# Slots of 511 rows instead of 383, and 42 instead of 44 node columns by slots and list, in a segment-max graph layer

## The chip, the cores and the metric

The kernel runs on one core of one Trainium2 chip. The metric is the device time of one execution in microseconds (us); the time before is 703.79 us, the median of 3 runs (703.43 to 704.61). A difference of 0.2% is 1.4 us.

## The reference, cut to what matters

There are 6250 nodes with 256 features each and 100,000 edges, sorted by their target `dst`. For every edge a message is made from its two ends, every node takes the maximum over the messages that arrive, and a layer norm follows.

```python
theta_x = (x[dst] - x[src]) @ theta_w.T + theta_b
phi_x = x[src] @ phi_w.T + phi_b
e = relu(theta_x + phi_x)
out = segment_max(e, dst, num_segments=6250)
out = where(isfinite(out), out, 0.0)
return layernorm(x + out)          # over the 256 features, no scale and no shift
```

The part of a message that depends on the target is the same for all of a node's edges. So it is enough to find, for every node, the maximum of B[src] over its edges, where B = x @ (phi_w - theta_w).T, and to add the target's part, the bias, the relu and the norm once per node.

## The kernel before, in words

**B.** TensorE (PE) makes the 6250 rows of B from transposed blocks of x (lines 771 to 815), and they are stored in DRAM as `b_rows`. Transposed x of the later nodes is kept in DRAM too (`x_columns`), for the end.

**Three ways to the maxima.** The nodes fall into two parts. The last P * TILES = 128 * 44 nodes (`OWN`, 5632 of them) are part 2; 44 consecutive nodes belong to each partition. The other `N1` = 618 nodes are part 1.

- *Part 1, by steps.* The first 128 * `FIRST_STEPS` edges are cut into 128 runs of 81 consecutive edges, one run to a partition. A step takes one edge of every run: GpSimd (POOL) gathers 128 rows of B into a `g` tile with one indirect DMA (`gather`, line 527, issued on line 528), and VectorE (DVE) does a running maximum that a cap cuts off where the node changes (line 696). Steps come in groups of 8 (`STEPS`) that fill one of five ring tiles (`RING`). The first two groups (`X_GROUPS`) gather x instead, before B is there. Each group is stored to `maxima_1`.
- *Part 2, by slots.* The 6250 rows of B are cut into slots of `SLOT_ROWS` = (KB - 1) * 128 + 127 = 383 rows: 16 full ones of three blocks and a last one of 122 rows in one block. For each slot, `choice` (line 1027) takes for every node of part 2 the lowest row of B in that slot among its edges of rank below 24 (`CHOICE_R`), two slots a batch, in int16 on DVE. The chosen row numbers are stored (`chosen_rows`) and read back broadcast to all partitions (`want`, line 1149). `make_hots` (line 1144) turns them into one-hot columns: an Abs and a Relu on ScalarE (ACT, lines 1157 and 1160), or one comparison on DVE for the first block (line 1155). `slot_halves` (line 1099) multiplies the slot's rows, split into two fp32r terms (`terms`), by the one-hot columns (line 1120), chunk by chunk of `CW` = 1024 nodes, in matmuls of 512 columns. A chunk has two halves of 128 features. A half's product is copied into `acc` for slot 0 (ACT, line 1132), and merged by a maximum for the others (DVE, line 1134).
- *Part 2, by list.* Edges that no slot took are packed into a list of 128 runs of `LIST_CHUNK` = 256 edges: `list_pieces` (line 1247) closes the gaps in eleven rounds on DVE (lines 1278 to 1288), stores `list_words`, and fetches each run again with three indirect DMAs (`gather_run`, line 540, each followed by a filler `iota` into `pause`). The list is then run like part 1: 256 gathers (`gather_2`, line 1346), 256 running maxima, stored to `maxima_2`; one last step carries over (line 694).

**Order.** Work is interleaved by hand (lines 1543 to 1665) and every engine works through its own queue in order. POOL's indirect DMAs are put in one order by `in_turn`: x, part 1, the three run gathers, the list (with the fix of part 1's heads, the list's carry and part 1's places between), part 2's places. From the 13th list piece on (`held`), each second gather waits for the running maximum that was queued last but one (`hold`, line 537). `halves_until` (line 1601) spreads the halves that are left evenly over the list's steps, all but those of `LAST_CHUNKS` parts. DVE's running maxima stay two groups (`LEAD`) behind the gathers.

**End.** When the list's maxima are stored, POOL gathers each node's row of `maxima_2` (one gather for each of the 44 columns), and shares of 8, 4 and 2 columns are finished: target's part on PE (line 1400), transposed `acc` (line 1409), maximum, sum and norm on DVE and ACT, store.

If a check on counts fails on the device, a general path sorts the edges and runs after all this (line 1671). It doesn't run here.

Of the kernel before, what the change touches and what calls it, by code (L numbers as in the profile page):

```python
# [39 lines left out]
FP = mybir.dt.float32  # L40
# [23 lines left out]
R = 36  # L64
ROWS = 127
KB = 3
SLOT = 512
DVE_HOTS = 1
SPREAD = 0.97
PAUSE = 160  # L70
CHOICE_R = 24
WORD = 1 << 13
# [363 lines left out]
def gnn_kernel(ctx: ExitStack, tc: tile.TileContext, x, src, dst, theta_w, theta_b, phi_w, phi_b, out):  # L436
# [19 lines left out]
    assert D == 2 * P and LEFT1 > 0 and OWN % 512 == 0 and TILES < 64 and P * T1 < E and WINDOW < E  # L456
    assert (P - 1) * T + 1 < E <= P * T and N < ID_MASK and P * T <= EDGES and E + 8 * P <= EDGES
    assert SLOT * NS <= slot_code(WORD - 1) < 1 << 15 and N < WORD and WORD << TABLE_BITS == 1 << 23 and SLOT == 1 << SLOT_BITS and P == 1 << P_BITS and SLOT_ROWS < SLOT and KB == 3 and ROWS == P - 1 and WINDOW <= 8 * P and OWN_LIST * P < 1 << 20
    BATCH_S = 2
    assert STEPS == 1 << STEPS_BITS and 3 * BATCH_S * CHOICE_R * TILES // 2 + TR <= 6 * WINDOW and LIST_CHUNK + 1 == LIST and LIST_CHUNK % STEPS == 0 and 3 * (BACK + LIST_CHUNK) <= WINDOW and BACK == R - 2 and CARRY_GROUPS * STEPS >= BACK and BACK + LIST_CHUNK <= OWN_LIST and R == 36 and CHOICE_R == 24 and OWN_LIST <= 512 and 1536 < TR <= 1536 + OWN_LIST  # L460

# [45 lines left out]

    pause = const.tile([P, PAUSE], FP, name="pause")
    latest = [None]
# [209 lines left out]
    slots = body.enter_context(tc.tile_pool(name="slots", bufs=2))  # L719
    weights = const.tile([P, KC, 2, D], FP, name="weights")  # L720

    bias_terms = const.tile([P, D], FR, name="bias_terms")
    pick = const.tile([P, P], FR, name="pick")
    with (
# [5 lines left out]
    ):  # L730
        w_in = prep.tile([P, 2, KC, D], FP, name="w_in")
        for i, w in enumerate((phi_w, theta_w)):
            nc.sync.dma_start(w_in[:, i], w.rearrange("(c p) k -> p c k", p=P))
        biases = prep.tile([P, 2, D], FP, name="biases")
        nc.vector.tensor_sub(w_in[:, 0], w_in[:, 0], w_in[:, 1])
        for i in range(2):
            for c in range(KC):
                ps = ps_t.tile([P, 2, KC, P], FP, name="ps_xt")
                for k in range(KC):
                    nc.tensor.transpose(ps[:, 0, k, :], w_in[:, i, c, k * P : (k + 1) * P], ident)  # L740
                weights_made = nc.vector.tensor_copy(weights[:, :, i, c * P : (c + 1) * P], ps[:, 0])
                if i == 1:
                    behind_in_order(weights_made, window_found[0], "search ahead of theta")
# [38 lines left out]
        def b_of(to, rows, kept=None):  # L782

            n = rows.shape[1]
            x_t = x_transposed(rows)
            if kept is not None:
                nc.sync.dma_start(kept, x_t[:, :n].rearrange("p h k n -> p (h k n)"))
            ps = ps_b.tile([P, 2, D], FP, name="ps_b")
            for h in range(n):
                for k in range(KC):  # L790
                    nc.tensor.matmul(  # L791
                        ps[:, h, :], x_t[:, h, k, :], weights[:, k, 0, :], start=(k == 0), stop=(k == KC - 1)
                    )
            nc.scalar.copy(to, ps[:, :n, :])  # L794
# [123 lines left out]
    def heads_1(capped):  # L918
        carry = misc()
        for k in range(KC):  # L920
            one = nc.tensor.transpose(carry[:, k * P : (k + 1) * P], capped[:, k, :], ident)
            behind_in_order(one, latest_product[0], "slots ahead of the heads")
        carried = work.tile([P, D], FP, name="carried", bufs=1)
# [4 lines left out]
        in_turn(iota(pause, 1, 0, 0))  # L928
        yield
# [11 lines left out]
    by_node = "p (j r) -> p j r"  # L941
    words, work_1, work_2, order = (table(n) for n in ("words", "work_1", "work_2", "order"))
    word = words.bitcast(I32)
# [3 lines left out]
    )  # L947
    behind_in_order(iota(order, 1, 1, 0), windows_fetched[0], "runs ahead of the ranks")
    padded, unused = table("padded", I16), table("unused", I16)
# [77 lines left out]
    def choice(s0):  # L1027
# [71 lines left out]
    def slot_halves(s, c):  # L1099
# [13 lines left out]
        for h in range(KC):  # L1113
            ps = ps_fetch.tile([P, CW], FP, name="ps_f")
            ps = ps[:, :wide_of]
            n = blocks * PARTS
            for i in range(n):
                b, part = divmod(i, PARTS)
                for w in range(0, wide_of, 512):
                    one = nc.tensor.matmul(  # L1120
                        ps[:, w : w + 512],
                        terms[:, part, b, h * P : (h + 1) * P],
                        hot[:, b, w : w + 512],
                        start=(i == 0),
                        stop=(i == n - 1),
                    )
# [3 lines left out]
            to = acc[:, h, begin : begin + wide_of]  # L1130
            if s == 0:
# [115 lines left out]
    def list_pieces():  # L1247
# [9 lines left out]
        node_ends = lambda row: row.rearrange(by_node, r=R)[:, :, R - 1]  # L1257
        nc.vector.tensor_tensor(up_to[:, 1:], node_ends(order), node_ends(before_it), op=ALU.subtract)
        yield
# [5 lines left out]
        )  # L1265
        distance = order.bitcast(I32)
        nc.vector.scalar_tensor_tensor(distance, empty, 0.5, before_it, op0=ALU.is_lt, op1=ALU.mult)
# [7 lines left out]
        for i in range((TR - 1).bit_length()):  # L1275
# [4 lines left out]
            )  # L1280
            if shift == 512:
                far = slice(3 * shift, TR)
                behind = slice(2 * shift, TR - shift)
                nc.vector.tensor_scalar(
                    moves[:, behind], done[:, far], 20 + i, 1, op0=ALU.logical_shift_right, op1=ALU.bitwise_and
                )
                nc.vector.copy_predicated(done[:, behind], moves[:, behind], done[:, far])
            one = nc.vector.copy_predicated(done[:, :n], moves[:, :n], done[:, shift : shift + n])  # L1288
# [14 lines left out]
        iota(edge, 1, 0, 0)  # L1303
        list_edges, second, third = (dst_w[:, i * n_run : (i + 1) * n_run] for i in range(3))
        for i, to in enumerate((list_edges, second, third)):
# [53 lines left out]
    def rows_of(part, j0, n, ps_tile):  # L1359
# [18 lines left out]
        def piece(k):  # L1378
            w = min(2, n - k)
            if part == 2:  # L1380
                j = j0 + k
                if j % 4 == 0:
                    x_tiles[0] = kept_ring.tile([P, 4 * KC, P], FP, name="kept")
                    rows = x_columns[:, j * KC * P : (j + 4) * KC * P]
                    nc.sync.dma_start(x_tiles[0], rows.rearrange("p (j n) -> p j n", n=P))
                x_t = x_tiles[0][:, j % 4 * KC :]
# [11 lines left out]
            for i in range(w):  # L1398
                for c in range(KC):
                    nc.tensor.matmul(  # L1400
                        a[:, i, :], x_t[:, 2 * i + c, :], weights[:, c, 1, :], start=False, stop=(i == w - 1 and c == KC - 1)
                    )
# [152 lines left out]
    for i, _ in enumerate(list_pieces()):  # L1555
# [8 lines left out]
        else:  # L1564
            fetch_parts(1)
    list_carry()
# [76 lines left out]
    assert widths[0] * P == CW  # L1643
    given, halves_of_tile = [0], []

    def by_turns():
# [4 lines left out]
        if not halves_of_tile:  # L1651
            both = ps_fetch.tile([P, CW], FP, name="ps_f")
            halves_of_tile.extend([both[:, : 2 * D], both[:, 2 * D :]])
        return halves_of_tile.pop(0)
# [47 lines left out]
```

## Time and profile before

| | us |
|---|---|
| median of 3 runs | 703.79 |
| the profiled execution's own time | 703.84 |
| its span in the profile | 702.0 |
| PE busy, weight loads aside | 650.7 |
| DVE busy | 627.0 |
| ACT busy | 513.2 |
| POOL busy | 438.1 |
| running maxima on DVE (line 696, 335 of them) | 161.1 |
| merges of slot products on DVE (line 1134, 192) | 216.4 |

Busy time of an engine leaves out issuing and waiting. POOL's 438.1 us are therefore not all the time for which its queue is taken: between two indirect DMAs that follow each other stands a gap that the profile calls "issue". A stage is best read by itself, since the stages have different limits: B until about 84 us, part 1 with the making of the list until about 225, the list until 598, and the end.

### The profile page before, as it was taken

To read this page: it belongs to the slowest core of one execution; us is meant where nothing else is said; L and a number is where in the kernel's file an instruction comes from. 1 tells how busy PE (TensorE), PEld (TensorE's weight loads), DVE (VectorE), ACT (ScalarE), POOL (GpSimd) and SP (SyncE) were. 2 spreads that over 40 slices of the span, in tenths; PEclk is the share of its full clock that TensorE was granted. 3 is DMA by queue.
4 is the path that set the end of the run, shared out by engine and by line. 5 is a ranking of instruction groups with operands and counts; after the bars stand their busy time and mean duration, and the time that the engine had idled before them with its cause. 6 is when DMAs were issued, how large, how long until landed. Compare 5 with 4: busy or idle time off the path is not lost.

```text
span 702.0 us, 9583 instructions
## 1 busy us (share of the span) xinstructions
PE 650.7 (93%) x2908; PEld 532.1 (76%) x2908; DVE 627.0 (89%) x1200; ACT 513.2 (73%) x597; POOL 438.1 (62%) x424
## 2 busy tenths in 40 slices
PE   4899978879798999999999999999999999999991
PEld 3688866657577788888888888888888878888881
DVE  6999999999998778989889897889888898979996
ACT  1345668989888877868778786779877687863596
POOL 6800178888813757777777677777667776057720
PEclk9899989989999999999999999999999999999996
DMA  8898563656645747868697689788887776655775
GB/s 249 293 350 322 191 187 109 204 192 210 215 174 182 260 150 255 266 225 284 209 319 241 219 302 332 230 247 280 307 267 262 247 235 208 206 170 162 261 292 206
DMA packets 61308, 167.04 MB, mean 238 GB/s; under 512 B 11944, under 2 KB 21953, under 8 KB 55233
## 3 DMA queue, kind: packets, MB, share of 16 engines
q1 hardware_dynamic: 40005, 106.89, 43.9%
q0 software_dynamic: 18976, 52.35, 25.1%
q10 hardware_dynamic: 2268, 7.11, 2.8%
q8 instruction: 25, 0.41, 0.3%
q14 instruction: 34, 0.28, 0.1%
HBM read 102.94 MB, written 63.36 MB: 237 GB/s over the span
## 4 chain that ended last, share of the span: by engine, by line
PE 61%; DVE 16%; ACT 7%; POOL 6%; issue 5%; DMA 4%; ACTq 0%; SPq 0%; DVEq 0%; POOLq 0%
PE ps_f L1120 58%; POOL g L528 6%; DVE words L1005 2%; ACT hot L1157 2%; ACT x_f L1458 2%; ACT hot L1160 2%; DMA g<-b_rows,src 1%; DVE work L1002 1%; DVE g L696 1%; ACT squares L1443 1%; DVE wide L1038 1%; DVE x_f L1414 1%; PE ps_e L1400 1%; DMA dst_w<-in_dst_dram,window 1%; DVE g L1410 1%
## 5 line engine op out<-in xcount | busy, mean ns | idle before, releaser
L1120 PE MATMUL ps_f<-hot,terms 128*128 128x512 f32 x2156 | 508.1, 396 | 18.8 <-DVE hot L1155 10.5
L1120 PEld LDWEIGHTS ps_f<-hot,terms 128*128 128x128 f32 x2156 | 406.6, 190 | 113.8 <-ACT hot L1160 14.6
L528 POOL DMA_INDIRECT g<-b_rows,list_src x256 | 262.4, 1025 | 107.8 <-issue 52.2
L1157 ACT ACTIVATE hot<-want,minus_row 128x1024 fp32r<-128x1024 f16 (+1 forms) x214 | 219.3, 1074 | 99.1 <-PE ps_f L1120 98.9
L1134 DVE TENSOR_TENSOR acc<-acc,ps_f 128x1024 f32<-128x1024 f32 x192 | 216.4, 1129 | 49.7 <-PE ps_f L1120 47.8
L1160 ACT ACTIVATE hot<-hot 128x2048 fp32r<-128x2048 f32 (+2 forms) x102 | 188.8, 1851 | 2.4
L696 DVE SCALAR_TENSOR_TENSOR g<-g,caps 128x256 f32<-128x256 f32 x335 | 161.1, 481 | 1.7
L528 POOL DMA_INDIRECT g<-b_rows,src x65 | 92.3, 1420 | 66.5 <-DMA b_rows<-b_sb 47.1
L791 PE MATMUL ps_b<-weights,x_t 128*128 128x256 f32 x260 | 63.7, 400 | 7.6 <-ACT x_t L779 7.2
L528 POOL DMA_INDIRECT g<-maxima,place x44 | 42.2, 960 | 33.7 <-DMA maxima<-g 20.6
L791 PEld LDWEIGHTS ps_b<-weights,x_t 128*128 128x128 f32 x260 | 50.4, 200 | 16.7 <-ACT x_t L779 10.1
L1155 DVE TENSOR_SCALAR hot<-want,row_id 128x1024 fp32r<-128x1024 f16 x80 | 56.9, 712 | 0.0
L794 ACT COPY b_sb<-ps_b 128x512 f32<-128x512 f32 (+1 forms) x25 | 14.4, 579 | 30.8 <-PE ps_b L791 21.1
L1400 PE MATMUL ps_e<-weights,kept 128*128 128x256 f32 x144 | 34.0, 379 | 0.0
L1443 ACT ACTIVATE squares<-x_f,r 128x256 bf16<-128x256 f32 x47 | 23.2, 494 | 12.5 <-DVE r L1440 12.5
L1400 PEld LDWEIGHTS ps_e<-weights,kept 128*128 128x128 f32 x144 | 27.3, 190 | 3.6
L528 POOL DMA_INDIRECT g<-in_x_dram,src x16 | 21.1, 1320 | 5.4 <-issue 4.1
L779 ACT COPY x_t<-ps_xt 128x512 f32<-128x512 f32 (+1 forms) x33 | 18.3, 590 | 7.8 <-PE ps_xt L776 7.6
L1458 ACT ACTIVATE x_f<-x_f,r 128x256 f32<-128x256 f32 x40 | 20.6, 587 | 4.6 <-DVE r L1450 4.6
L1288 DVE COPY_PREDICATED work<-words,work 128x316 int32<-128x316 int32 (+9 forms) x11 | 18.2, 1659 | 0.0
L1414 DVE SCALAR_TENSOR_TENSOR x_f<-g,x_f 128x256 f32<-128x256 f32 x44 | 17.1, 423 | 0.3
L1038 DVE TENSOR_TENSOR wide<-wide 128x88 int16<-128x88 int16 (+5 forms) x45 | 16.2, 360 | 1.3
(273 smaller groups left out, 405.8 us busy)
## 6 DMA issues: line engine op xcount, KB each, us to landing
maxima<-g SPq DMA_DIRECT2D x41, 1024.0 KB
want<-chosen_rows SPq DMA_DIRECT2D x85, 256.0 KB
x_q<-in_x_dram SPq DMA_DIRECT2D x12, 512.0 KB
b_rows<-b_sb ACTq DMA_DIRECT2D x12, 512.0 KB
x_columns<-x_t SPq DMA_DIRECT2D x22, 256.0 KB
kept<-x_columns SPq DMA_DIRECT2D x11, 512.0 KB
raw<-b_rows SPq DMA_DIRECT2D x16, 256.0 KB
g<-b_rows,list_src POOLq DMA_INDIRECT x256, 4.9
```

What stands on the lines that cost most here:

```text
L528: one = nc.gpsimd.indirect_dma_start(out=to, out_offset=None, in_=table, in_offset=bass.IndirectOffsetOnAxis(ap=offsets, axis=0))
L696: one = nc.vector.scalar_tensor_tensor(g[:, k, :], last[part], caps[:, t : t + 1], g[:, k, :], op0=ALU.min, op1=ALU.max)
L791: nc.tensor.matmul(ps[:, h, :], x_t[:, h, k, :], weights[:, k, 0, :], start=(k == 0), stop=(k == KC - 1))
L1120: one = nc.tensor.matmul(ps[:, w : w + 512], terms[:, part, b, h * P : (h + 1) * P], hot[:, b, w : w + 512], start=(i == 0), stop=(i == n ...
L1134: one = nc.vector.tensor_tensor(to, to, ps, op=ALU.max)
L1155: nc.vector.tensor_scalar(hot[:, b, :], want, row_id[:, b : b + 1], None, op0=ALU.is_equal)
L1157: nc.scalar.activation(hot[:, b, :], want, AF.Abs, bias=minus_row[:, b : b + 1], scale=1.0)
L1160: nc.scalar.activation(apart, apart.bitcast(FP), AF.Relu, bias=1.0, scale=-1.0)
L1400: nc.tensor.matmul(a[:, i, :], x_t[:, 2 * i + c, :], weights[:, c, 1, :], start=False, stop=(i == w - 1 and c == KC - 1))
L1414: one = nc.vector.scalar_tensor_tensor(y, m[:, i, :], 0.0, y, op0=ALU.max, op1=ALU.add, accum_out=totals[:, i : i + 1])
L1443: nc.scalar.activation(squares, x_f[:, k, :], AF.Square, bias=mean[:, k : k + 1], scale=1.0, accum_out=var[:, k : k + 1])
L1458: nc.scalar.activation(x_f[:, k, :], x_f[:, k, :], AF.Identity, bias=mean[:, k : k + 1], scale=inv[:, k : k + 1])
```

## The change

Constants first. Slots get four blocks (`KB`), so 511 rows: 12 full ones and a last one of 118 rows. Part 2 has 42 columns (5376 nodes), cut into six chunks of 896, each in two matmuls of 448 columns that stand at the starts of two PSUM banks. Part 1 has 874 nodes and 112 steps in 14 groups. The list has 304 steps and one that carries over. Ranks below 20 are offered to the slots.

```diff
-AHEAD_OF_RUNS = 3
+AHEAD_OF_RUNS = 2
-FIRST_STEPS = 81
+FIRST_STEPS = 112
-TILES = 44
-LIST = 257
-WINDOW = 872
+TILES = 42
+LIST = 305
+WINDOW = 848
-KB = 3
+KB = 4
-PAUSE = 160
-CHOICE_R = 24
+CHOICE_R = 20
-LAST_CHUNKS = 10
+LAST_CHUNKS = 9
-OWN_LIST = 316
-LIST_CHUNK = 256
+OWN_LIST = 368
+LIST_CHUNK = 304
...
-    CW = 1024
+    CW = 896
```

The filler after each run gather and after the gather of heads goes:

```diff
         indirect(to, flat(table, 0, [[total, 1], [1, total]]), bass.IndirectOffsetOnAxis(ap=offsets, axis=1))
-        in_turn(iota(pause, 1, 0, 0))
```

The matmuls of a half:

```diff
-            ps = ps_fetch.tile([P, CW], FP, name="ps_f")
-            ps = ps[:, :wide_of]
+            ps = ps_fetch.tile([P, 2, 512], FP, name="ps_f")
+            half = wide_of // 2
+            ps = ps[:, :, :half]
...
-                for w in range(0, wide_of, 512):
+                for w in range(2):
                     one = nc.tensor.matmul(
-                        ps[:, w : w + 512],
+                        ps[:, w, :],
                         terms[:, part, b, h * P : (h + 1) * P],
-                        hot[:, b, w : w + 512],
+                        hot[:, b, w * half : (w + 1) * half],
```

The choice over 20 ranks, its minimum taken in five steps as before:

```diff
-        least(low, in_slot[:, :n, : 12 * W], in_slot[:, :n, 12 * W :])
-        least(low[:, :, : 6 * W], low[:, :, : 6 * W], low[:, :, 6 * W :])
-        least(low[:, :, : 3 * W], low[:, :, : 3 * W], low[:, :, 3 * W : 6 * W])
+        least(low, in_slot[:, :n, : 10 * W], in_slot[:, :n, 10 * W :])
+        least(low[:, :, : 5 * W], low[:, :, : 5 * W], low[:, :, 5 * W :])
+        least(low[:, :, : 2 * W], low[:, :, : 2 * W], low[:, :, 2 * W : 4 * W])
         least(low[:, :, :W], low[:, :, :W], low[:, :, W : 2 * W])
-        least(low[:, :, :W], low[:, :, :W], low[:, :, 2 * W : 3 * W])
+        least(low[:, :, :W], low[:, :, :W], low[:, :, 4 * W : 5 * W])
```

In the loop over the list's pieces, an odd piece brings one half instead of two while groups of part 1 are left. In the list's round of distance 512 the two instructions for far elements go (lines 1284 and 1287). At the end, `widths` loses its last share of 2:

```diff
-            fetch_parts(1)
+            fetch_half()
+            if len(groups_1) == 0 and i < 13:
+                fetch_half()
...
-    while halves_left[0] > 2 * (len(CHUNKS) - 1):
+    while halves_left[0] > 2 * (len(CHUNKS) - 2):
...
-    widths = [STEPS] * 3 + [4, 4, 4, 4, 2, 2]
+    widths = [STEPS] * 3 + [4, 4, 4, 4, 2]
```

Otherwise, phi's transposed weights stand in a tile of the first stage (`weights_b`), the table `order` shrinks to one number per column (`node_top`), and two buffers take the place of others that are done with.

More of the change, by code (lines that the diff above doesn't have):

```diff
@@ L731, in gnn_kernel @@
         w_in = prep.tile([P, 2, KC, D], FP, name="w_in")
+        weights_b = prep.tile([P, KC, D], FP, name="weights_b")
         for i, w in enumerate((phi_w, theta_w)):
@@ L922, in heads_1 @@
             behind_in_order(one, latest_product[0], "slots ahead of the heads")
-        carried = work.tile([P, D], FP, name="carried", bufs=1)
+        carried = work.tile([P, KC, P], FP, name="tails", bufs=1).rearrange("p k n -> p (k n)")
         nc.scalar.copy(carried, carry[:, :D])
@@ L941, in gnn_kernel @@
     by_node = "p (j r) -> p j r"
-    words, work_1, work_2, order = (table(n) for n in ("words", "work_1", "work_2", "order"))
+    words, work_1, work_2 = (table(n) for n in ("words", "work_1", "work_2"))
     word = words.bitcast(I32)
@@ L947, in gnn_kernel @@
     )
-    behind_in_order(iota(order, 1, 1, 0), windows_fetched[0], "runs ahead of the ranks")
+    node_top = index.tile([P, TILES], FP, name="node_top")
+    behind_in_order(iota(node_top, R, R, 0), windows_fetched[0], "runs ahead of the ranks")
     padded, unused = table("padded", I16), table("unused", I16)
@@ L1129, in slot_halves @@
                 hots_of[parts[0]] = make_hots(*parts[0])
-            to = acc[:, h, begin : begin + wide_of]
+            to = acc[:, h, begin : begin + wide_of].rearrange("p (w n) -> p w n", w=2)
             if s == 0:
@@ L1265, in list_pieces @@
         )
-        distance = order.bitcast(I32)
+        distance = before_it.bitcast(I32)
         nc.vector.scalar_tensor_tensor(distance, empty, 0.5, before_it, op0=ALU.is_lt, op1=ALU.mult)
@@ L1303, in list_pieces @@
         iota(edge, 1, 0, 0)
-        list_edges, second, third = (dst_w[:, i * n_run : (i + 1) * n_run] for i in range(3))
+        list_edges, second = (dst_w[:, i * n_run : (i + 1) * n_run] for i in range(2))
+        third = src_w[:, :n_run]
         for i, to in enumerate((list_edges, second, third)):
@@ L1400, in piece @@
                     nc.tensor.matmul(
-                        a[:, i, :], x_t[:, 2 * i + c, :], weights[:, c, 1, :], start=False, stop=(i == w - 1 and c == KC - 1)
+                        a[:, i, :], x_t[:, 2 * i + c, :], weights[:, c, :], start=False, stop=(i == w - 1 and c == KC - 1)
                     )
@@ L1639, in gnn_kernel @@
         pass
-    widths = [STEPS] * 3 + [4, 4, 4, 4, 2, 2]
+    widths = [STEPS] * 3 + [4, 4, 4, 4, 2]
     assert sum(widths) == TILES
     last_shares = [(2, sum(widths[:i]), n) for i, n in enumerate(widths)]
-    assert widths[0] * P == CW
+    assert widths[0] * P <= 2 * CW and 2 * D == 512
     given, halves_of_tile = [0], []
@@ L1651, in by_turns @@
         if not halves_of_tile:
-            both = ps_fetch.tile([P, CW], FP, name="ps_f")
-            halves_of_tile.extend([both[:, : 2 * D], both[:, 2 * D :]])
+            both = ps_fetch.tile([P, 2, 512], FP, name="ps_f")
+            halves_of_tile.extend([both[:, 0, :], both[:, 1, :]])
         return halves_of_tile.pop(0)
```

28 lines of the change are left out of this document (10 added, 18 removed).

## The prediction

> **What bounds the kernel now.** I read the busy times by stage first, then the groups that carry a stage, then POOL's timeline.
>
> ```profile
> core 0: us, PE busy (x) PEld busy (x) DVE busy (x) ACT busy (x) POOL busy (x), PEclk, DMA share, GB/s
> ...
> 84.00:196.00 112.00, 91.76 (x367) 72.55 (x366) 109.20 (x202) 91.99 (x110) 92.63 (x66) 0.89 0.59 184
> ...
> 225.00:598.00 373.00, 372.59 (x1640) 304.02 (x1639) 325.16 (x539) 291.84 (x254) 270.42 (x265) 1.00 0.77 254
> ...
> sum 702.00, PE 650.68 PEld 532.14 DVE 627.04 ACT 513.22 POOL 438.13; mean PE 108.45 PEld 88.69 DVE 104.51 ACT 85.54 POOL 73.02
> ```
>
> ```profile
> L1120 PE MATMUL ps_f<-hot,terms 128*128 128x512 f32 x2156 | 508.1, 396 | 18.8 <-DVE hot L1155 10.5
> L1120 PEld LDWEIGHTS ps_f<-hot,terms 128*128 128x128 f32 x2156 | 406.6, 190 | 113.8 <-ACT hot L1160 14.6
> L528 POOL DMA_INDIRECT g<-b_rows,list_src x256 | 262.4, 1025 | 107.8 <-issue 52.2
> L1157 ACT ACTIVATE hot<-want,minus_row 128x1024 fp32r<-128x1024 f16 (+1 forms) x214 | 219.3, 1074 | 99.1 <-PE ps_f L1120 98.9
> L1134 DVE TENSOR_TENSOR acc<-acc,ps_f 128x1024 f32<-128x1024 f32 x192 | 216.4, 1129 | 49.7 <-PE ps_f L1120 47.8
> L1160 ACT ACTIVATE hot<-hot 128x2048 fp32r<-128x2048 f32 (+2 forms) x102 | 188.8, 1851 | 2.4
> L696 DVE SCALAR_TENSOR_TENSOR g<-g,caps 128x256 f32<-128x256 f32 x335 | 161.1, 481 | 1.7
> L528 POOL DMA_INDIRECT g<-b_rows,src x65 | 92.3, 1420 | 66.5 <-DMA b_rows<-b_sb 47.1
> ```
>
> In the list stage (225 to 598 us) PE is busy 372.59 of 373.00 us: the slots' matmuls bound it. POOL shows 270.42 us there and looks idle for a quarter. It isn't. The next fences have the list gathers' durations (minimum / median / maximum, ns) and rows of POOL's timeline (start, length, what, idle before):
>
> ```profile
> L528 POOL DMA_INDIRECT g<-b_rows,list_src x256: 942/948/1672, 224.8 to 596.8; - x128
> ```
>
> ```profile
> 83.93 1.10 POOL L528 DMA_INDIRECT g<-b_rows,src  x1 [47.10 <-DMA b_rows<-b_sb]
> ...
> 195.06 0.95 POOL L528 DMA_INDIRECT g<-b_rows,src  x1 [0.31 <-issue]
> 212.66 1.10 POOL L521 DMA_INDIRECT dst_w<-list_words,run_start  x1 [16.66 <-DMA list_words<-work]
> 213.77 0.30 POOL L498 IOTA pause<- 128x160 f32 x1
> ...
> 215.65 0.96 POOL L521 DMA_INDIRECT dst_w<-list_words,run_start  x1 [0.16 <-issue]
> ...
> 224.80 1.14 POOL L528 DMA_INDIRECT g<-b_rows,list_src  x1 [7.91 <-DVE list_src L1314]
> ...
> 596.77 1.02 POOL L528 DMA_INDIRECT g<-b_rows,list_src  x1 [0.30 <-issue]
> 618.35 0.94 POOL L528 DMA_INDIRECT g<-maxima,place  x1 [20.57 <-DMA maxima<-g]
> 619.60 0.95 POOL L528 DMA_INDIRECT g<-maxima,place  x1 [0.30 <-issue]
> 620.85 0.94 POOL L528 DMA_INDIRECT g<-maxima,place  x1 [0.30 <-issue]
> ```
>
> No list gather takes under 942 ns, and 0.30 us of issue follow a gather even where nothing is waited for: from 619.60 to 620.85 it is 1.25 us. So 1.246 us a gather (0.942 + 0.304) is the least that I count on, and with the list's mean of 1.025 it is 1.33. The list stage holds 264 indirect DMAs (256 of the list, 8 of heads, carry and part 1's places) in 373 us, 1.41 each: PE holds POOL back by only 0.08 us a gather, some 21 us. That is all the room POOL has there.
>
> **The matmuls.** Both kernels have 49 blocks, so the columns fall as 5376 to 5632: 2156 matmuls of 512 become 2352 of 448. Now 508.1 / 2156 is 0.2357 us each. What 64 columns less save is bounded by nothing (0.2357 us stays: 554.4 us in all) and by proportion (0.2062: 485.0 us). I take the slope between two fp32r widths, since it is measured:
>
> ```profile
> L1397 PE MATMUL ps<-bias_terms,pick 128*128 128x512 f32 x5 | 2.0, 395 | 0.0
> ...
> L1397 PE MATMUL ps<-bias_terms,pick 128*128 128x256 f32 x1 | 0.3, 280 | 0.0
> ```
>
> (395 - 280) / 256 = 0.449 ns a column, so 0.2357 - 0.0288 = 0.2069 us and 486.7 us in all: 21 us less for PE. DVE has 144 merges instead of 192 (at most 1.129 us each, so at least 54 us less) and 79 more running maxima (38 us more). ACT and DVE make 294 one-hot blocks before and after, now narrower. Neither engine becomes the bound.
>
> **POOL's queue** gets 31 + 48 = 79 more gathers, 105 us at 1.33, and loses two places and the fillers. It is in one order, so I follow it from the moment B is stored.
>
> 1. B is ready at 83.9 as now, since its work stays the same.
> 2. 65 gathers take 83.93 to 196.01, 112.1 us. Of the 14 groups, 11 stand ahead of the run gathers as now, the last with 8 steps instead of one: 7 more at 1.420 + 0.304, 12.1 us. At 208.1.
> 3. The run gathers wait for `list_words`, which land at 212.66 now because DVE, which makes them, is busy for 109.20 of 112 us. Its choice goes from nine batches to seven, each over 20 * 42 instead of 24 * 44 numbers, so 38% of the 46.23 us that DVE spends here on the choice's tile `wide` go, 17.6 us:
>
> ```profile
> 62.00:127.00 65.00, 46.23 (x97) 0.40 (x1) 0.92 0.55 178
> ```
>
>    I take the words to be there by 208; without that cover it costs up to 4.6 us. The three run gathers take 3.95 us now (212.66 to 216.61), 0.9 of it fillers that go: 3.1. At 211.2.
> 4. New in the queue: part 1's last three groups, 24 gathers, behind the run gathers and ahead of the whole list. Every second one waits for a running maximum of the group before. 24 * 1.33 = 31.9. At 243.1.
> 5. The list's first gathers wait for part 1's last maxima: a landing (4.9, below) and one step (0.5). At 248.5, with the whole list queued behind. But these maxima are queued on DVE among the merges, up to the 45th half, and PE may be later.
>
> ```profile
> 101.30 6.48 PE ps_f L1120 x24
> ...
> 615.36 2.26 DMA maxima<-g
> ```
>
> ```profile
> g<-b_rows,list_src POOLq DMA_INDIRECT x256, 4.9
> ```
>
>    The first half starts at 101.3 (chain row). Up to the 30th half ACT makes all blocks: (219.3 + 188.8) / 214 = 1.91 us a block, times 0.875 for 896 columns, 6.7 us a part of four, over the matmuls' 6.6. 15 parts take 100, the 12 copies of slot 0 (at 1.074 * 0.875) 11, three first chunks save 1.7 each for DVE's block, and 7.5 more parts take 50 at PE's price: 156, at 257. Between 248.5 and 257 I take the middle, 253, as the trace of before shows neither order on DVE. Today's list starts at 224.8.
> 6. 304 list gathers at 1.33 are 404.3, 10 others (heads 2, carry 1, places of part 1 now 7) at 1.25 are 12.5: at 669.8. Today it is 597.8. PE is no bound there: of 156 halves 45 are ahead and 18 behind, and 93 * 16 * 0.2069 is 308 of 417 us.
> 7. From the last list gather to the first place it takes 20.6 us now (597.79 to 618.35). With PE no longer late there remain a landing (4.9), eight steps (3.8), the carry's step (0.4), and the store with its issue (615.36 to 618.35, 3.0): 12.1. At 681.9.
> 8. From the first place to the end it is 83.65 us now, minus two gathers (2.5): 81.15. Span 763.
>
> Around the span lie 703.84 - 702.0 = 1.8 us; the profiled execution stands 0.05 us over the median. **Forecast 765 us.** PE's 21 us and DVE's 16 are hidden under POOL's queue; behind POOL nothing else is late until the places.
>
> Bounds: with the 7, 24 and 304 gathers of steps 2, 4 and 6 at 1.246 and step 5 without PE it is 765 - 4.5 - 3.4 - 27.6 = 730; the smaller choice can also take up to a fifth off what lengthens step 2's other gathers (65 * 0.47 * 0.2 = 6): 724. With step 5 at 257, step 7 at today's 20.6, and the list half-way to today's 1.41 (12.6), it is 790.
>
> **A rule on the price of a gather.** The gathers' mean is 1420 ns while the list is made, 1025 in the list, where the median is 948, and 0.95 us among the places: something lengthens some of them. The Trainium skill, SBUF — State Buffer, "Who interferes with whom", says that a DVE instruction with two SBUF inputs, or in a two-port mode, shuts GpSimd out for its whole length. The running maximum of line 696 has two, and there is one for each list gather before and after; by that rule 1.33 stays, and the places' 0.95, with hardly such steps beside them, agree. If the price went with DVE's busy share instead (325 of 373 us now; 16 us less over 417 then), it would be 1.31 and the sum some 7 us lower.
>
> **Rivals.**
> - *The matmuls stay the bound, faster.* PE's 372.59 of 373.00 us speak for it. Then the end comes 21.4 us of matmuls and two places earlier: 680 us. It needs POOL's path to take 63 us less over those 345 gathers, 0.18 each, so 1.15 us a gather, and no list gather of the trace is under 942 + 304 ns. It decides only if the waits of steps 3 to 5 and the lengthened gathers vanish together. Chance 0.07.
> - *A matmul costs the same at 448 columns*, because its weight load of 190 ns doesn't shrink. PE then needs 46 us more, 750 by itself; with POOL's queue beside it some 775. Against it: loads overlap one another. 72 loads of the transposes at 141 ns would fill 10.2 us and take 9.0:
>
> ```profile
> L1409 PEld LDWEIGHTS ps_e<-ident,acc 128*128 128x128 f32 x72 | 9.0, 141 | 1.8
> ```
>
>    Chance 0.05, inside the range.
> - *PE's clock falls as PE idles.* From 84 to 196 us PE idles 18% and its granted clock is 0.89. In the new list stage PE idles 26%, and it becomes the bound there under 308 / 417 = 0.74 of the clock; at half the clock the stage takes 616 us, and the time is 964. The Trainium skill, TensorE: Matmul & The Clock Gate, "HAM oscillation — how this bites in real kernels", has half the clock behind gaps over some 3.4 us. The trace's 0.89 speaks against so deep a fall. Chance 0.02.
> - *It breaks its own limits*, so the general path runs too. Counted on the inputs, part 1 has 13,785 edges for 14,336 places and the list 38,008 for 38,912. I give it no chance.
>
> **How the numbers follow.** POOL's queue as the bound gets 0.86, the two other slower cases 0.05 and 0.02, faster 0.07. Of the first, 0.03 could still end within 0.2% of before, about what a measurement of this kernel can tell from no change. So faster 0.07, same 0.03, slower 0.90. The range holds both bounds, 724 to 790.
>
> **What would show it.** In the changed kernel's profile: list gathers back to back, 304 in 395 to 430 us from near 253; PE under 80% busy in that stage; POOL instead of line 1120 as the larger part of the chain; line 1120 near 0.207 us a matmul; the first place near 682. It is wrong if list gathers follow each other by less than 1.24 us, if the list starts before 225, or if PE is busy throughout.

## The result and the profile after

The changed kernel takes **785.6 us** (median of 4 runs, 782.88 to 787.78) beside 704.18 us for the kernel before (4 runs, 703.43 to 704.61): a ratio of **1.116, 95% interval 1.112 to 1.120**. It is slower, as forecast, and 20.6 us over the forecast of 765, inside its range. The profiled execution took 784.49 us, with a span of 782.6. Ratios here and below leave out executions that a disturbance lengthened, so they aren't always the quotients of the medians.

Busy time by stage, cut where the forecast's steps 2, 4, 6 and 7 end:

```profile
core 0: us, PE busy (x) PEld busy (x) DVE busy (x) ACT busy (x) POOL busy (x), PEclk, DMA share, GB/s
...
84.00:207.00 123.00, 96.61 (x433) 85.41 (x432) 100.78 (x213) 101.64 (x119) 101.20 (x74) 0.90 0.62 197
207.00:249.00 42.00, 25.94 (x98) 22.38 (x98) 26.74 (x66) 23.66 (x23) 26.84 (x27) 0.76 0.72 235
249.00:697.00 448.00, 400.06 (x1876) 359.90 (x1876) 302.09 (x520) 319.82 (x264) 313.05 (x314) 0.96 0.73 233
```

The list stage grew from 373 to 448 us. TensorE filled all of it before; now it is idle for 48 us of it. Ahead of it stands a stage that didn't exist (207 to 249 us, the 24 new gathers of part 1), in which every engine is idle for a third of the time or more. The groups that carry the sum:

```profile
L1120 PE MATMUL ps_f<-hot,terms 128*128 128x448 f32 x2352 | 521.5, 383 | 80.3 <-DVE acc L1134 40.7 <-DVE hot L1155 28.6 <-ACT hot L1160 10.9
L526 POOL DMA_INDIRECT g<-b_rows,list_src x304 | 302.8, 996 | 136.4 <-issue 66.1 <-DVE g L693 59.9 <-DMA g<-b_rows,list_src 6.4
L693 DVE SCALAR_TENSOR_TENSOR g<-g,caps 128x256 f32<-128x256 f32 x414 | 200.1, 483 | 132.0 <-DMA g<-b_rows,list_src 93.2 <-DMA g<-b_rows,src 23.5 <-issue 10.2
L1134 DVE TENSOR_TENSOR acc<-acc,ps_f 128x896 f32<-128x896 f32 x144 | 155.3, 1082 | 43.2 <-PE ps_f L1120 42.8
```

The third row is the sign that the roles have changed: DVE's running maxima wait 93.2 us for list gathers to land. In the list stage of before, DVE waited for TensorE and for no gather. The matmuls' idle time has also grown, and its first entry is new: they wait for DVE's merges (line 1134). POOL's timeline (start, length, what, idle before) shows the forecast's steps one by one:

```profile
205.48 0.95 POOL L526 DMA_INDIRECT g<-b_rows,src  x1 [0.30 <-issue]
206.73 0.94 POOL L519 DMA_INDIRECT dst_w<-list_words,run_start  x1 [0.30 <-issue]
...
209.23 0.95 POOL L519 DMA_INDIRECT src_w<-list_words,run_start  x1 [0.30 <-issue]
212.18 0.94 POOL L526 DMA_INDIRECT g<-b_rows,src  x1 [2.01 <-DVE g L693]
...
243.01 0.95 POOL L526 DMA_INDIRECT g<-b_rows,src  x1 [0.30 <-issue]
249.41 1.08 POOL L526 DMA_INDIRECT g<-b_rows,list_src  x1 [5.46 <-DVE g L693]
...
272.48 1.19 POOL L526 DMA_INDIRECT g<-b_rows,list_src  x1 [0.30 <-issue]
312.04 1.14 POOL L526 DMA_INDIRECT g<-b_rows,list_src  x1 [38.38 <-DVE g L693]
...
695.48 0.95 POOL L526 DMA_INDIRECT g<-b_rows,list_src  x1 [0.31 <-issue]
707.59 0.95 POOL L526 DMA_INDIRECT g<-maxima,place  x1 [11.16 <-issue]
```

| end of step | forecast us | measured us |
|---|---|---|
| 2, the 72 gathers | 208.1 | 206.4 |
| 3, the run gathers | 211.2 | 210.2 |
| 4, the last 24 gathers of part 1 | 243.1 | 244.0 |
| 5, first list gather | 253 | 249.4 |
| 6, last list gather | 669.8 | 696.4 |
| 7, first place | 681.9 | 707.6 |
| 8, end of the span | 763 | 782.6 |

Up to 249 us every step is within 4 us. Then one row holds what was not foreseen: after 18 list gathers **POOL stands still for 38.38 us**. No buffer is missing there, since the 19th gather goes into a tile of the ring that has taken two gathers already. It is the kernel's own `hold` (line 535): every second gather waits for the running maximum that was queued last but one, and for the 19th that is the list's second maximum. It ends at 311.78, and the gather starts at 312.04. The kernel before has the same wait at the same gather, but a short one:

```profile
254.48 1.21 POOL L528 DMA_INDIRECT g<-b_rows,list_src  x1 [4.76 <-DVE g L696]
```

DVE's timeline in the changed kernel says why the maximum is late:

```profile
248.66 1.02 DVE L693 SCALAR_TENSOR_TENSOR g<-g,caps 128x256 f32<-128x256 f32 x2 [1.39 <-DMA g<-b_rows,src]
249.59 2.08 DVE L1134 TENSOR_TENSOR acc<-acc,ps_f 128x896 f32<-128x896 f32 x2
...
254.94 1.09 DVE L1134 TENSOR_TENSOR acc<-acc,ps_f 128x896 f32<-128x896 f32 x1 [2.17 <-PE ps_f L1120]
258.19 1.09 DVE L1134 TENSOR_TENSOR acc<-acc,ps_f 128x896 f32<-128x896 f32 x1 [2.15 <-PE ps_f L1120]
...
306.83 1.09 DVE L1134 TENSOR_TENSOR acc<-acc,ps_f 128x896 f32<-128x896 f32 x1 [1.56 <-PE ps_f L1120]
307.83 0.48 DVE L693 SCALAR_TENSOR_TENSOR g<-g,caps 128x256 f32<-128x256 f32 x1
...
311.30 0.48 DVE L693 SCALAR_TENSOR_TENSOR g<-g,caps 128x256 f32<-128x256 f32 x1
```

DVE works through its queue in order, and the kernel puts each maximum of the list behind the merge that was queued last (lines 700 and 701). Between the last two maxima of the early gathers (248.66) and the list's first (307.83) stand 19 merges, and nearly each waits for its half: they come every 3.24 us (254.94 to 258.19), 16 matmuls at 0.203 us. The list's gathers land unused behind them. Merges done by the time that the list starts, first before (to 225 us), then after (to 249 us), each with the line's matmuls in that time:

```profile
L1134 DVE TENSOR_TENSOR acc<-acc,ps_f x24: 683/1207/1221, 153.6 to 224.4; 128x1024 f32<-128x1024 f32 x20, 128x512 f32<-128x512 f32 x4
...
L1120 PE MATMUL ps_f<-hot,terms x401: 387/389/792, 101.3 to 224.9; 128*128 128x512 f32 x134
```

```profile
L1134 DVE TENSOR_TENSOR acc<-acc,ps_f x14: 1071/1080/1121, 161.3 to 242.2; 128x896 f32<-128x896 f32 x14
...
L1120 PE MATMUL ps_f<-hot,terms x448: 358/368/743, 101.3 to 243.6; 128*128 128x448 f32 x150
```

A half was 12 matmuls (6 in the narrow last chunk) and is 16 now, four blocks instead of three. With the 12 halves of slot 0, which are copied and not merged, 36 of the 44 halves ahead of the list's first maximum were done when the list started. The 8 that were left came every 2.7 us, 22 us, and the 19 DMAs that POOL could issue ahead cover 24 us at 1.25. Now the 448 matmuls are 28 of 45 halves. The 17 left are 272 matmuls, 55 us at 0.203, and 249.4 + 55 is 304: the last merge is at 306.83.

### The profile page after: what moved, and what is told of

The parts are those of the page before. It is cut to its first block, busy times and chain, and to the rows that moved or that the text cites. A ratio compares the mean times of both kernels' runs of the same rounds, so it can differ in the third digit from the quotient of the medians.

```text
span 782.6 us, 10023 instructions
## 1 busy us (share of the span) xinstructions
PE 660.7 (84%) x3106; PEld 586.4 (75%) x3106; DVE 575.5 (74%) x1173; ACT 530.3 (68%) x599; POOL 508.8 (65%) x497
## 5 line engine op out<-in xcount | busy, mean ns | idle before, releaser
L1120 PE MATMUL ps_f<-hot,terms 128*128 128x448 f32 x2352 | 521.5, 383 | 80.3 <-DVE acc L1134 40.7
L1120 PEld LDWEIGHTS ps_f<-hot,terms 128*128 128x128 f32 x2352 | 462.1, 198 | 132.6 <-issue 40.4
L526 POOL DMA_INDIRECT g<-b_rows,list_src x304 | 302.8, 996 | 136.4 <-issue 66.1
L1157 ACT ACTIVATE hot<-want,minus_row 128x896 fp32r<-128x896 f16 x235 | 228.9, 1038 | 123.3 <-PE ps_f L1120 122.1
L693 DVE SCALAR_TENSOR_TENSOR g<-g,caps 128x256 f32<-128x256 f32 x414 | 200.1, 483 | 132.0 <-DMA g<-b_rows,list_src 93.2
L1160 ACT ACTIVATE hot<-hot 128x2688 fp32r<-128x2688 f32 (+2 forms) x78 | 191.9, 2460 | 1.7
L1134 DVE TENSOR_TENSOR acc<-acc,ps_f 128x896 f32<-128x896 f32 x144 | 155.3, 1082 | 43.2 <-PE ps_f L1120 42.8
L790 PE MATMUL ps_b<-weights_b,x_t 128*128 128x256 f32 x260 | 61.7, 391 | 6.3 <-ACT x_t L778 6.0
L790 PEld LDWEIGHTS ps_b<-weights_b,x_t 128*128 128x128 f32 x260 | 49.2, 195 | 14.8 <-ACT x_t L778 8.6
L1155 DVE TENSOR_SCALAR hot<-want,row_id 128x896 fp32r<-128x896 f16 x59 | 41.5, 703 | 3.1 <-DMA want<-chosen_rows 3.1
```

The lines of the kernel that those rows point to most:

```text
L526: one = nc.gpsimd.indirect_dma_start(out=to, out_offset=None, in_=table, in_offset=bass.IndirectOffsetOnAxis(ap=offsets, axis=0))
L693: one = nc.vector.scalar_tensor_tensor(g[:, k, :], last[part], caps[:, t : t + 1], g[:, k, :], op0=ALU.min, op1=ALU.max)
L790: nc.tensor.matmul(ps[:, h, :], x_t[:, h, k, :], weights_b[:, k, :], start=(k == 0), stop=(k == KC - 1))
L1120: one = nc.tensor.matmul(ps[:, w, :], terms[:, part, b, h * P : (h + 1) * P], hot[:, b, w * half : (w + 1) * half], start=(i == 0), stop=( ...
L1134: one = nc.vector.tensor_tensor(to, to, ps, op=ALU.max)
L1155: nc.vector.tensor_scalar(hot[:, b, :], want, row_id[:, b : b + 1], None, op0=ALU.is_equal)
```

## The experiments

The theory: POOL's queue sets the time, so the 79 added gathers are paid in full, and the slots' side of the change costs through the stop. The rival, in different shapes: the matmuls set it. The experiments were measured in three sets, each on another chip, and in all three the kernel before itself took 807 to 812 us instead of 704. So only ratios to the kernel before of the same set are used, and microseconds are worked out from them. Where an expectation for one of the first eight runs names microseconds of a whole run, it reckons from 704, and is read as a ratio here. "The stop" is POOL's wait ahead of the 19th list gather; one expectation calls it the 17th.

**Gathers only.** The kernel before with the changed counts of gathers; slots, columns and matmuls stay (one run gather writes into another buffer, to make room).

```diff
-FIRST_STEPS = 81
+FIRST_STEPS = 112
-LIST = 257
+LIST = 305
-OWN_LIST = 316
-LIST_CHUNK = 256
+OWN_LIST = 368
+LIST_CHUNK = 304
```

> Before's slots (383 rows, 44 columns, matmuls of 512) with the changed kernel's 112 first steps and 304 list steps: 79 gathers more, nothing else. POOL's queue as the bound: list gathers start near 250 us as in the changed kernel, 304 follow at 1.30 or more, first place at 680 or later; 765 to 810 us, since the matmuls too are before's. If the new shape of the slots is the cost instead: under 725 us, with POOL filling idle time.

> The kernel of e1 again (before's slots, 112 first steps, 304 list steps), on a chip that runs before in 704 us. POOL's queue as the bound: the list starts near 250 us, 304 gathers at 1.30 or more and a stop while the matmuls are late, 770 to 815 us. If the slots' new shape is the cost: under 725 us.

Measured: 900.04 us beside 808.21, ratio 1.111 (1.105 to 1.118), and 905.03 beside 811.79, ratio 1.120 (1.110 to 1.130). So 90 and 97 us for 79 gathers, 1.14 and 1.23 us each: the gathers alone, with the slots and columns of before, make nearly the whole loss. Both ratios lie in the range expected for POOL's queue (1.09 to 1.16), though the list starts at 271 and 276 us and not near 250. The stop is short here:

```profile
310.64 1.07 POOL L528 DMA_INDIRECT g<-b_rows,list_src  x1 [9.38 <-DVE g L696]
```

**Slots only.** The changed kernel with the old counts of gathers; edges that find no place are left out.

```diff
-FIRST_STEPS = 112
+FIRST_STEPS = 81
-LIST = 305
+LIST = 257
-OWN_LIST = 368
-LIST_CHUNK = 304
+OWN_LIST = 316
+LIST_CHUNK = 256
```

> The changed kernel's slots (511 rows in four blocks, 42 columns, matmuls of 448) with before's 81 first steps and 256 list steps; edges that do not fit are left out, and the check on counts is taken out, so the work of the list is cut, not the slots'. POOL's queue as the bound: it has before's length again, the matmuls are 20 to 30 us shorter, 670 to 695 us. If the slots' shape is the cost: over 720 us.

> The kernel of e2 again (the changed slots and columns, before's 81 first and 256 list steps, so edges are left out). POOL's queue as the bound: 665 to 700 us. If the slots' shape is the cost: over 720 us.

Measured: 813.66 us beside 808.21, ratio 1.006 (1.001 to 1.010), and 819.17 beside 811.79, ratio 1.015 (1.006 to 1.024). Neither case of the expectations came: they gave 0.94 to 0.99 with POOL's queue as the bound, over 1.02 with the slots' shape as the cost. The cheaper matmuls bring nothing in these sets even without the added gathers (at 704 us it wasn't tried). POOL's queue shows where the gain went: with these slots the list starts at 214.5 us and its last gather at 673.0; in the kernel before of the last set, at 227.5 and 663.1. The list starts 13 us earlier and ends 10 later, and the stop is 22.5 us longer (slots only, then before):

```profile
280.92 1.15 POOL L526 DMA_INDIRECT g<-b_rows,list_src  x1 [42.73 <-DVE g L693]
```

```profile
271.90 1.21 POOL L528 DMA_INDIRECT g<-b_rows,list_src  x1 [20.18 <-DVE g L696]
```

So the longer stop comes with the slots, not with the added gathers. Of its 22.5 us, 13 are the list's earlier start.

**Twelve halves later.** The changed kernel whole, but the last three groups of part 1 bring no halves, so that 33 instead of 45 stand ahead of the list.

```diff
     while groups_1 or todo or searched[0] is not None:
-        next_group_1(2)
+        next_group_1(0)
```

> The changed kernel with 12 halves fewer queued ahead of the list (33 instead of 45), left to the list's steps. In the changed kernel POOL stops for 38.4 us at the 17th list gather, which waits for a running maximum that stands on DVE behind the merges of late matmuls. If that stop adds to the queue's length: it goes, and the time is 740 to 755 us. If the list only starts over and pays later (PE then being the bound): 775 to 788 us.

> The kernel of e3 again (12 halves moved from ahead of the list into it). If POOL's stop of 38.4 us adds to the queue's length: 740 to 760 us, the stop under 10 us. If it is paid elsewhere: 775 to 790 us.

Measured: 895.19 us, ratio 1.104 (1.097 to 1.111), and 888.74, ratio 1.102 (1.091 to 1.113). As a ratio to before this is the second case of the expectations (1.10 to 1.12, the stop paid elsewhere) and not the first (1.05 to 1.08). But the whole change has 1.132 in the last set (below). Beside that, compared across sets, it is 0.03 less, some 24 us, and the stop has shrunk to 13.70 and 11.58:

```profile
288.84 1.15 POOL L526 DMA_INDIRECT g<-b_rows,list_src  x1 [11.58 <-DVE g L693]
```

The stop is thus on the path, and its length follows the number of halves in front, but of the 40 us that it lost only some 24 reach the end. The traces show where most of the rest is: POOL's other waits ahead of list gathers for running maxima add up to 86.7 us here (98.3 less the stop of 11.58) and to 71.2 in the whole change of the last set (124.6 less 53.42). The halves moved into the list hold the gathers up there. This form is better than the change as it stands, and still 10% slower than before.

**42 columns, slots of 383 rows.** The changed kernel with the old three-block slots and a list of 248 steps.

```diff
-KB = 4
+KB = 3
-LIST = 305
+LIST = 249
-OWN_LIST = 368
-LIST_CHUNK = 304
+OWN_LIST = 316
+LIST_CHUNK = 248
```

> The changed kernel with slots of 383 rows again (three blocks, 17 slots) and so 248 list steps; 42 columns, 112 first steps and matmuls of 448 stay. POOL's queue: 56 list gathers fewer, 73 us at 1.30, first place near 600 to 615 and, PE being about as late, 675 to 705 us, at or under before. If part 1's 31 steps with their place ahead of the list are the main cost: over 730 us.

> The kernel of e4 again (changed kernel with slots of 383 rows and so 248 list steps). POOL's queue: 56 gathers fewer than changed, some 73 us, and 17 slots give the matmuls the same length: 680 to 715 us. If part 1's 31 steps ahead of the list are the main cost: over 730 us.

Measured: 825.72 us (810.43 to 839.54) beside 808.21, and 825.28 (812.59 to 834.51) beside 811.79. The runs scatter too far for an interval: by the fastest runs of each it is 1.01, by the medians 1.02. That is above the first expectation for POOL's queue (0.96 to 1.00), about the upper end of the second (0.97 to 1.02), and under the 1.04 of the rival. With 23 gathers more than before it loses little, and there is no stop: in the second trace POOL's waits from 250 to 345 us have 10.8 us for running maxima, none over 3.0.

```profile
POOL g L526 <- DVE g L693: 10.8, 9, 3.0
```

All 33 merges are done by 253.6 us here, although the 112 first steps and 42 columns are those of the change. With slots only, where the stop is there without the added gathers, this points to the fourth block.

**The whole change again, and its two kinds of gathers taken back singly.** The second and third leave out the edges that find no place.

```diff
-LIST = 305
+LIST = 257
-OWN_LIST = 368
-LIST_CHUNK = 304
+OWN_LIST = 316
+LIST_CHUNK = 256
```

```diff
-FIRST_STEPS = 112
+FIRST_STEPS = 81
```

> The changed kernel itself, next to the kernel before of the same call, so that gathers only (1.111 and 1.120), slots only (1.006 and 1.015), halves later (1.104 and 1.102) and 42 columns with slots of 383 rows stand beside the whole change at one place. Theory (GpSimd's queue of gathers sets the end, and its stop of 38.4 us at the first list maximum is paid once): the ratio stays at about 1.116 where the kernel before takes 704 us; where it takes 808 to 812 us as in the two calls before, the added 79 gathers are still about 80 to 95 us, so 1.10 to 1.12, and the stop is 40 us or more. Rival (the matmuls set the end once TensorE is slow): TensorE's 2352 pairs instead of 2156 at 9 in 10 of the time per pair cancel, and the ratio falls to 1.02 to 1.06.

> The changed kernel with a list of 256 steps in place of 304; edges that no longer find a place are left out, so 48 of the 79 added gathers and their running maxima fall away and the slots, columns and first steps stay as changed. Theory (GpSimd's queue sets the end): 48 times 1.30 us, some 62 us, less than the whole change: a ratio lower by 0.07 to 0.09 than the whole change in the same call. Rival (the matmuls bind as soon as the list is shorter: TensorE was busy for 400 of the 448 us of the list stage): no more than some 40 us less, a ratio lower by 0.03 to 0.055.

> The changed kernel with 81 first steps in place of 112; edges that no longer find a place are left out, so 31 of the 79 added gathers and their running maxima fall away and slots, columns and list stay as changed. Theory (each added gather is paid on GpSimd's queue, and the stop at the first list maximum stays or shrinks because TensorE is held less by the running maxima of the first steps): 31 times 1.30 us, some 40 us, or more: a ratio lower by 0.05 to 0.07 than the whole change. Rival (until the 45th half is merged TensorE sets the pace, whatever the first steps take): the stop of GpSimd grows by what the gathers save, the 45 halves end as late as now, and the ratio is lower by less than 0.02.

Measured side by side, beside 809.42 us:

| kernel | us | ratio, 95% interval | stop in its trace, us |
|---|---|---|---|
| whole change | 920.64 | 1.132 (1.125 to 1.139) | 53.42 |
| list of 256 steps | 862.83 | 1.055 (1.046 to 1.063) | 58.82 |
| 81 first steps | 873.37 | 1.074 (1.065 to 1.084) | 42.18 |

The ratio of the whole change came out above what theory and rival named; the stop is over 40 us as the theory had it. Taking 48 list gathers back lowers the ratio by 0.077, 63 us of 809 or 1.31 a gather; taking 31 first gathers back lowers it by 0.058, 47 us or 1.50 a gather. Both are in the theory's range and outside the rival's. Together they are 0.135, the whole change 0.132, and slots only (0.006 and 0.015) and gathers only (0.111 and 0.120) add up to 0.117 to 0.135: the two sides of the change hardly help or hinder each other. That a first gather costs more than a list gather goes with the stop, which is 11.2 us shorter without them (35 us, 1.14 each, without that). It is shorter with 33 instead of 45 halves ahead, and still there since the list also starts 49 us earlier:

```profile
272.62 1.15 POOL L526 DMA_INDIRECT g<-b_rows,list_src  x1 [42.18 <-DVE g L693]
```

**The kernel before again.**

> The kernel before against itself: a ratio of 1.000 within 0.01, and its trace at the place of these runs. Theory (the place, and not the kernels, makes the 15% where the kernel before takes 808 us): the same gathers, matmuls and running maxima, with TensorE's gaps that no semaphore ends and a lower granted clock. Rival (the time of the call was that of a disturbed run alone): about 704 us, with the trace as it was.

Measured: 807.23 us, ratio 0.996 (0.992 to 1.000). All ten runs lie between 803 and 813 us, so it isn't a single run that was long: as the theory has it, the same 9583 instructions take 15% longer here, with TensorE's waits changed and a granted clock of 0.93 instead of 0.97. Two rows of TensorE's waits, the slots' weight loads and matmuls held up by nothing that the profile shows:

```profile
PEld ps_f L1120 <- issue: 77.1, 23, 25.6
```

```profile
PE ps_f L1120 <- issue: 38.4, 12, 25.4
```

At 704 us the kernel before has 11.9 us in the first of these. The list stage takes 437 instead of 373 us, and from the first place to the end it is 126 instead of 84. What holds TensorE there wasn't tried and stays open; in the whole change that row has 179.0 us. That may be why the ratio is 1.132 there and 1.116 in the first measurement, but no run separates it.

## Why the prediction was right, and where it was off

**The bound was right.** POOL's queue took the place of the matmuls. The runs with the gathers alone (1.11 and 1.12), the two that take them back (0.077 and 0.058) and DVE's 93.2 us of waiting for landings all say so. Behind the stop POOL's queue is full: from 312 to 697 us it holds 295 DMAs of 294.29 us in all, and with 0.305 of issue each that is 384.3 of 385.0 us, while TensorE is busy for 337.79:

```profile
312.00:697.00 385.00, 337.79 (x1576) 302.18 (x1574) 271.89 (x484) 272.09 (x228) 294.29 (x295) 0.96 0.79 254
```

The forecast's 105 us for 79 gathers stands beside 90 to 97 us for adding them and 109 for taking them back. In the profile of the changed kernel the list's mean of 996 ns with 0.305 of issue is 1.30; 314 DMAs at that price are 408 us, and the 447.0 of the list less the stop are 408.6. Two of the named signs missed: the list took 447 us where 395 to 430 were given, because of the stop, and TensorE is busy for 89% of it where under 80% were given. The share of the chain of waits, which was to show POOL too, can't be read: the chain breaks off at its first step in this trace.

**Steps 2, 3, 4 and 7 held**, to 1.9 us or better each, and 11.16 us for step 7's gap where 12.1 were given. The run gathers waited for nothing (0.30 us of issue), so the smaller choice hid the list's words, as step 3 had taken it. The 24 gathers of step 4 took 31.8 us, 31.9 forecast, behind a wait of 2.0 us for a running maximum.

**Step 5 failed.** It saw maxima queued on DVE among the merges up to the 45th half, but took them for part 1's last ones, and put the 45th half at 257 us. Part 1's last maxima ran at 249, ahead of 19 of the merges. It was the list's own maxima that stood behind the 45th half, and that was merged at 307. The forecast let the first 30 halves run at ACT's and TensorE's pace, 6.7 us for two, and had them done by about 207; the trace has 28 by 249. It left out that the halves of this stage are written in between the groups of part 1, so that a merge stands on DVE in line with running maxima that wait for POOL's gathers. TensorE's and DVE's waits from 84 to 249 us, which from 84 to 225 us of before were 0.2 us for the first, 0.6 for the second and none for the third:

```profile
PE ps_f L1120 <- DVE acc L1134: 23.1, 5, 10.5
```

```profile
PEld ps_f L1120 <- DVE acc L1134: 12.3, 5, 7.1
```

```profile
DVE g L693 <- DMA g<-b_rows,src: 23.5, 16, 5.3
```

That this alone held the halves back is not shown. TensorE's clock did its part: from 84 to 249 us it was at half for some 44 us, and TensorE was busy for 30 of them, which at the full clock would have been 15 by proportion, an estimate. Before, from 84 to 225 us, it was 24 us, 21 of them busy. The forecast had no term for that in step 5. In the last set's trace of the whole change the same 14 merges are done by 256 us, but there TensorE waits for ACT's blocks (19.7 us on its matmuls, 22.3 on its loads) and in gaps of issue, and not for merges. Shown is the rest: 28 halves instead of 45, and a stop that shrinks as halves are taken from in front.

Step 5 also looked for the price at the wrong place: as a later first list gather. That one came early, at 249.4, and the wait struck 18 gathers on, at the first `hold` on a maximum of the list. Of the error of 19.6 us in the span the stop is +38.4; against it stand the earlier list (-3.6), its gathers at 1.30 instead of 1.33 (-8.2), the gap before the places (-0.9) and the end behind them (-6.1: 75.0 us where 81.15 were given). The last is unexplained by any run: after the last place it is 22.1 us to the end instead of 28.3. These four are 18.8 us together; with the stop alone the time would have come to some 803 us, over the range's 790. That it lies inside is in part luck.

**The price of a matmul** was right where nothing waits, 0.203 us for 0.207 forecast (16 to a half of 3.24 us). In part that is luck: the forecast took its slope off a mean of 0.2357 that held stalls, and where nothing waited before it was 0.227 (12 to a half of 2.72 us), which would have given 0.198. The changed group's mean of 0.2217 (521.5 / 2352) holds stalls as well. The list stage has TensorE busier than forecast all the same, 89% instead of 74%, since more of the halves were left for it (1824 of the matmuls where 93 halves, 1488, were forecast); so its margin under POOL is thinner than the forecast had it.

**The rivals.** A matmul didn't cost the same at 448 columns. The limits were kept. The clock did fall to one half where TensorE idled, but only for stretches: behind the idle gap of 10.5 us that ends at 214.20 it was 0.50, and 1.00 again from 220 us (columns as in the first fence; the clock stands third from the end).

```profile
214.00:218.00 4.00, 3.80 (x10) 3.48 (x11) 4.00 (x16) 0.00 (x0) 2.60 (x4) 0.50 0.32 91
220.00:224.00 4.00, 4.00 (x21) 3.64 (x20) 3.49 (x8) 1.45 (x6) 3.08 (x4) 1.00 0.87 259
```

This agrees with the half clock of the Trainium skill's section on HAM oscillation (TensorE: Matmul & The Clock Gate). The stages' means of 0.76 (207 to 249 us) and 0.96 (the list) mix stretches at 1.0 and at 0.5, and so did the 0.89 of before, which the forecast took as a sign against a fall to half. What was right is that the list stage doesn't run at half throughout: there it is some 38 of 448 us.

The faster rival needed 1.15 us a gather by the forecast; its sum isn't clear, since from 765 to 680 us are 85 us, 0.25 for each of 345, which asks for 1.08. In the changed kernel's profile, too, no gather came under 942 ns and 0.304 of issue.

**The rule on GpSimd and DVE** (the Trainium skill, SBUF — State Buffer, "Who interferes with whom") has a DVE instruction with two SBUF inputs contend with a GpSimd instruction that reads SBUF. A running maximum has two, and a gather's row numbers (`list_src`) lie in SBUF. The traces agree, with the list gathers sorted by what DVE did during each:

| DVE beside the gather | before: gathers, mean (longest) ns | after: gathers, mean (longest) ns |
|---|---|---|
| nothing, or merges alone | 42, 947 (977) | 67, 945 (951) |
| running maxima, with or without merges | 94, 992 (1201) | 139, 982 (1201) |
| a one-hot comparison (line 1155), with or without the others | 82, 1108 (1492) | 69, 1043 (1402) |
| other work | 38, 1014 (1672) | 29, 1069 (1969) |

A merge, with one input in SBUF and one in PSUM, lengthens nothing, so the price doesn't go with DVE's busy share. It didn't stay at 1.33 either: with fewer gathers beside comparisons and more beside nothing, the mean fell from 1025 to 996 ns. The table shows what goes together; no run takes one of these instructions away.

## What to carry to other kernels

Where two engines are nearly level, price an exchange of work between them on the one that is not named the bound: here TensorE was busy all the time, but POOL had 21 us of room in the list stage, and the change put 48 gathers there, 64 us at 1.33, and 31 more ahead of it. When a unit of work is made larger, the places at which a given number of units is put ahead of something else have to be counted again in work: the halves ahead of the list were some 500 matmuls (401 and 8 times 12) and are 720. And a late engine is felt at the first instruction that is made to wait for its results, not where the stage begins: here that is 18 gathers on, at a `hold` that the kernel itself sets. Whether POOL would gain without it wasn't tried.

## What the runs showed that was not expected

- fp32r matmuls of 448 columns follow each other by 0.203 us in the stretch from 255 to 307 us (3.24 us for 16), although each has a weight load of its own, 186 ns long at the least (median 188).
- The granted clock of TensorE is either whole or half in these traces, and a stage's mean hides which: 0.76 is half of it for 20 of 42 us.
- A list gather beside merges alone is as short as one beside an idle DVE (951 ns at the most in the changed kernel); beside a one-hot comparison it takes 1043 ns in the mean.
- The same program, with the same instructions, took 15% longer in three later sets of runs (807 to 812 us instead of 704), with gaps on TensorE that end on no semaphore in the trace, and a change that costs 81 us at 704 costs 0.132 of 809, 107 us, there.
- An added indirect gather costs between 1.14 and 1.50 us of the whole kernel's time, whichever run takes it out or puts it in; the shortest list gather in any of the profiles is 0.940 us long.
